# A Mamba layer and linear attention on one core: the C product taken once per four scans

## The chip, the cores and the metric

The kernel runs on one core of a Trainium2 chip. The core has a matrix engine (TensorE, PE in the profile), a vector engine (VectorE, DVE), an activation engine (ScalarE, ACT), a general engine (GpSimd, POOL) and a queue engine that here only issues DMAs (SyncE, SP). Each engine takes its instructions strictly in the order in which the program gives them, and waits for the others through semaphores. The metric is the device time of one execution in microseconds (us); the median of three runs of the kernel before is 8079.81 us.

## What is computed

`x` has 4 images of 512 channels and 4096 positions. Layer 0 normalises it, cuts the channels into 4 chunks of 128 and sends each chunk through a Mamba block, along the 4096 positions. Its core is a recurrence for each of 256 inner channels `d` and 16 states `s`:

```
dA = exp(dt_t[:, :, None] * A)
h  = dA * h + (dt_t * x_t)[:, :, None] * B_t[:, None, :]
y  = einsum('bds,bs->bd', h, C_t)
```

The y of all positions, plus a skip term, is gated, projected, normalised and projected again, and added to x. Layer 1 is a linear attention over the result (relu of q and k, k·q summed over the positions, then the output projection). Both layers are fp32.

## The kernel before

**Steps and slots.** The work is cut into 128 steps: 4 images x 8 tiles of 512 positions x 4 chunks. A step has 16 slots (`SLOTS`), numbered s = 0 to 15 here, and a slot has two scans: the recurrence over 512 positions for a block of 128 pairs of channel and state, one instruction each. Two slots make a group of four scans that shares four states; a group has one tile `h` of four rows of 512 columns, of which two buffers exist. The first slot of a group is even, the second odd. Below, "scan 4a" and "scan 4b" are the two scans of slot 4, and "P4" is slot 4's C product.

**What one slot needs.** `dA` is made by ScalarE into PSUM (`decay`, L709, three buffers, given out three scans ahead). `bx`, the input term of a slot's two scans, is made by GpSimd (`drive`, L718, three buffers, two slots ahead). VectorE runs the scans (L740). Then h must be multiplied by C. C is split by columns: for the first 384 of the 512 columns (`CUT`) TensorE spreads the C rows of the group's four states over the partitions into a PSUM tile `c_all` (`c_row`, L703, one buffer), and VectorE multiplies (`product`, L758, L763); for the last 128 columns the rows come by DMA into `c_sb`, and GpSimd multiplies all four rows of h at once (L751), after it has copied the state at the end of the scans (`st`, L750). Last, TensorE adds the product up over the states into `y` (`fold_states`, L769), eight matmuls for a group, in PSUM.

**The order.** It is written out by hand: the function `slot` (L726) gives a slot's instructions to the engines, and calls `after()` (L1114) at its end. `after()` gives out a share of all other work: the softplus of the next step at s = 3 (two table loads on ScalarE around it), the silu at s = 10 (again two), TensorE's input projections at s = 3 and 5 to 9, and pieces of the layer norms, the output projection and the attention, as many as a credit of matmul work per slot allows. The wide VectorE instructions of the layer norms (2048 columns) come at s = 3 and s = 10 (`AWAY`).

**Where the product stands.** A product takes one slot: two rows of 384 columns, 768 in all. It is given out one scan late: slot g's product follows the first scan of slot g + 1, and with it, if g is odd, the C rows of the next group and the state sums of this one. In slots 4 and 11 (`BEHIND`) the slot's own product comes as well, at its end, so these two slots have two products, the second just behind the scan that it reads, and slots 5 and 12 have none.

**PSUM and its one C tile.** Since `c_all` has one buffer, TensorE may write the next group's C rows only when VectorE has done the group's second product, and the next product needs them.

Of the kernel before, what the change touches and what calls it, by code (L numbers as in the profile page):

```python
# [11 lines left out]
ALU = mybir.AluOpType  # L12
# [12 lines left out]
def kernel(  # L25
# [24 lines left out]
    nc = tc.nc  # L50
# [7 lines left out]
    CUT = T - T // 4  # L58
# [3 lines left out]
    NJ = P // BLK  # L62
# [58 lines left out]
    def mm(out_, lhsT, rhs, abreast=1, **how):  # L121

        work["mm"] += (0.25 if rhs.dtype == BF16 else 1.0) * rhs.shape[-1] / T / abreast
        nc.tensor.matmul(out_, lhsT, rhs, **how)  # L124
# [3 lines left out]
    def diagonal(out_, w, rhs):  # L128

        for k in range(P // BLK):  # L130
            r = slice(k * BLK, (k + 1) * BLK)
            mm(out_[r, :], w[r, :], rhs[r, :], abreast=P // BLK, start=True, stop=False)
# [242 lines left out]
    def bc(v, n):  # L375
        return v.unsqueeze(1).to_broadcast([P, n, v.shape[-1]])
# [296 lines left out]
    JJ = NJ // 2  # L673
    SLOTS = NH * NQ * JJ
    AWAY = (3, 10)
    BEHIND = [s + 1 for s in AWAY]

    def place(g):

        n, r = divmod(g, SLOTS)  # L680
        e, r = divmod(r, NQ * JJ)
        return n, e, *divmod(r, JJ)

    b_all, c_all, c_sb, dAs, bxs, hs, ys = {}, {}, {}, {}, {}, {}, {}
# [8 lines left out]
    def b_row(g):  # L693
        n, e, q, _ = place(g)
        b_all[g // JJ] = wk.tile([P, T], F32, tag="b_all", name=f"b_all_{g}", bufs=3)
        for_states(b_all[g // JJ], fs[n]["b_rows"], q)

    def c_tail(g):
        n, e, q, _ = place(g)
        c_sb[g // JJ] = wk.tile([P, T - CUT], F32, tag="c_sb", name=f"c_sb_{g}", bufs=2)  # L700
        for_states(c_sb[g // JJ], fs[n]["c_rows"], q)

    def c_row(g):  # L703
        n, e, q, _ = place(g)
        got = ps_c.tile([P, CUT], F32, tag="c", name=f"c_all_{g}")
        mm(got, sel[:, q, :], fs[n]["parts"], start=True, stop=True)
        c_all[g // JJ] = got

    def decay(k):  # L709

        n, e, q, jj = place(k // 2)
        j = jj * 2 + k % 2
        dAs[k] = ps_d.tile([P, T], F32, tag="dA", name=f"dA_{k}")
        nc.scalar.activation(  # L714
            dAs[k], fs[n]["d_all", e][:, 0, j, :], AF.Exp, scale=a_t[:, e, j, q : q + 1]
        )

    def drive(g):  # L718

        n, e, q, jj = place(g)  # L720
        bxs[g] = wk.tile([P, 2, T], F32, tag="bx", name=f"bx_{g}", bufs=3)
        nc.gpsimd.tensor_tensor(  # L722
            bxs[g], fs[n]["d_all", e][:, 1, jj * 2 : jj * 2 + 2, :], bc(b_all[g // JJ], 2), ALU.mult
        )

    def slot(g, last, after):  # L726
        n, e, q, jj = place(g)
        b, t, c = steps[n]
        if g + 2 < last:
            drive(g + 2)  # L730
        if jj == 0:
            if g + 3 * JJ < last:
                b_row(g + 3 * JJ)
            hs[g // JJ] = wk.tile([P, NJ, T], F32, tag="h", name=f"h_{g}", bufs=2)
        elif g + 1 < last:
            c_tail(g + 1)
        h = hs[g // JJ]
        for i in range(2):
            j = jj * 2 + i
            nc.vector.tensor_tensor_scan(  # L740
                h[:, j, :], dAs.pop(2 * g + i), bxs[g][:, i, :],
                0.0 if t == 0 else st[:, c, e, q, j : j + 1], ALU.mult, ALU.add,
            )
            if 2 * g + i + LEAD < 2 * last:
                decay(2 * g + i + LEAD)
            if i == 0 and g and (g - 1) % SLOTS not in BEHIND:
                product(g - 1, last)
        del bxs[g]
        if jj == JJ - 1:
            nc.gpsimd.tensor_copy(st[:, c, e, q, :], h[:, :, T - 1])  # L750
            nc.gpsimd.tensor_tensor(  # L751
                h[:, :, CUT:], h[:, :, CUT:], bc(c_sb.pop(g // JJ), NJ), ALU.mult
            )
        if g % SLOTS in BEHIND:
            product(g, last)
        after()

    def product(g, last):  # L758


        _, _, _, jj = place(g)
        own = hs[g // JJ][:, jj * 2 : jj * 2 + 2, :CUT]
        nc.vector.tensor_tensor(own, own, bc(c_all[g // JJ], 2), ALU.mult)  # L763
        if jj == JJ - 1:
            if g + 1 < last:
                c_row(g + 1)
            fold_states(g)

    def fold_states(g):  # L769

        n, e, q, _ = place(g)
        if q == 0:
            ys[n, e] = ps_y.tile([P, T], F32, tag="y", name=f"y_{n}_{e}")
            diagonal(ys[n, e], dg[:, e, :], fs[n]["xz"][:, 0, e, :])
        h = hs.pop(g // JJ)
        for j in range(NJ):
            mm(
                ys[n, e][j * BLK : (j + 1) * BLK, :], fold, h[:, j, :],
                start=False, stop=(q == NQ - 1), abreast=NJ,
            )  # L780
# [232 lines left out]
    N = len(steps)  # L1013
# [86 lines left out]
    with tc.manual_schedule():  # L1100
        credit, seen, mix, held[0], held_x[0] = 0.0, work["mm"], iter(()), 0, 0
        for n, (b, t, c) in enumerate(steps):
# [10 lines left out]
            for s in range(SLOTS):  # L1113
                def after():  # L1114
# [62 lines left out]
                    seen = work["mm"]  # L1177

                slot(n * SLOTS + s, N * SLOTS, after)
            fs[n - 1].clear() if n else None  # L1180
        product(N * SLOTS - 1, N * SLOTS)
        now[0] = None
        for _, what in due:
            what()
# [60 lines left out]
```

## Time and profile before

| | value |
|---|---|
| median of 3 runs | 8079.81 us (8078.26 to 8084.43) |
| the profiled execution, its span | 8075.2 us |
| before the loop of slots, the loop, after it | 123, 7485, 468 us |
| one slot, mean (7485 / 2048) | 3.65 us |
| one scan, mean of L740 with `st` | 1271 ns |
| one C product on VectorE (L763) | 935 ns, 2048 of them |
| one `bx` on GpSimd (L722) | 2371 ns, 2048 of them |
| one C product of the tail on GpSimd (L751) | 1270 ns, 1024 of them |

The profile is of one execution. "Busy" sums the durations of an engine's instructions; neighbours on VectorE overlap by some 85 ns, so what an instruction takes of the engine's time is read as the distance from its start to the start of the next, in the timeline. A bracket in a timeline line gives the idle time before the instruction and what ended it.

### The profile page before, as it was taken

The page shows a single profiled execution, that of the slowest core. Times are in us where ns is not written, and L with a number is a line of the kernel's source. Part 1 is how long each engine was busy: PE and PEld are TensorE (multiplying, and loading weights), DVE is VectorE, ACT ScalarE, POOL GpSimd, SP SyncE. Part 2 cuts the span into 40 slices and gives each one's busy share as a digit, 9 for nine tenths or more (in the row PEclk, how much of TensorE's full clock was granted, in tenths as well). Part 3 has the DMA queues.
Part 4 walks back from the last instruction along what each step waited for, and adds up shares of the span by engine and source line. Part 5 has one row for each costly group of instructions (what it writes and reads, how often), then busy time and mean ns, then how long its engine had stood idle before and what let it go on. Part 6 is the DMA issues. An engine that isn't in the chain of part 4 may idle for free.

```text
span 8075.2 us, 92673 instructions
## 1 busy us (share of the span) xinstructions
PE 6509.7 (81%) x24880; PEld 2130.1 (26%) x24880; DVE 7049.8 (87%) x6790; ACT 5543.1 (69%) x8321; POOL 6890.9 (85%) x4597
## 2 busy tenths in 40 slices
PE   5677777667788888887788888888788888888599
PEld 1111212111223222332222222322122222322144
DVE  5999999999999989989999999998989999998600
ACT  4667777777777677777777767777776777777421
POOL 4999999999989888989998889898989999889600
PEclk7787888888899999898899999999889999999799
DMA  5666666666666666676766666677666666677402
GB/s 158 165 168 163 148 152 154 157 157 165 169 171 161 146 155 160 172 188 170 173 152 168 165 151 157 156 183 186 159 159 155 159 154 150 155 189 186 114 32 89
DMA packets 829200, 1266.00 MB, mean 157 GB/s; under 512 B 183912, under 2 KB 317560, under 8 KB 816384
## 3 DMA queue, kind: packets, MB, share of 16 engines
q1 hardware_dynamic: 804736, 1222.32, 60.3%
q0 software_dynamic: 16896, 33.56, 2.4%
q10 hardware_dynamic: 7040, 4.20, 0.2%
q8 instruction: 195, 3.19, 0.2%
q14 instruction: 333, 2.73, 0.1%
HBM read 1052.78 MB, written 206.57 MB: 156 GB/s over the span
## 4 chain that ended last, share of the span: by engine, by line
DVE 21%; PE 19%; DMA 17%; POOL 14%; issue 10%; ACT 9%; SPq 8%; POOLq 0%; DVEq 0%; ACTq 0%
DVE h L740 13%; POOL bx L722 10%; DMA d_all<-d_rows 10%; DVE h L763 6%; PE pq L124 5%; SPq L689 5%; ACT dA L714 4%; PE pc L124 3%; DMA b_all<-b_rows 3%; SPq L639 3%; PE y L124 2%; PE pr L124 2%; POOL h L751 2%; DMA c_sb<-c_rows 2%; PE pp L124 1%
## 5 line engine op out<-in xcount | busy, mean ns | idle before, releaser
L722 POOL TENSOR_TENSOR bx<-d_all,b_all 128x1024 f32<-128x1024 f32 x2048 | 4819.3, 2371 | 64.6 <-DVE h L740 48.0
L740 DVE TENSOR_TENSOR_SCAN h<-dA,st,bx 128x512 f32<-128x512 f32 x3584 | 4431.9, 1271 | 114.8 <-ACT dA L714 105.0
L714 ACT ACTIVATE dA<-d_all,a_t 128x512 f32<-128x512 f32 x4096 | 2779.7, 689 | 1761.3 <-DVE h L740 1720.6
L763 DVE TENSOR_TENSOR h<-h,c_all 128x768 f32<-128x768 f32 x2048 | 1914.8, 935 | 328.6 <-PE c_all L124 320.4
L124 PE MATMUL y<-h,fold 128*32 128x512 f32 x8192 | 1264.7, 693 | 196.6 <-POOL h L751 193.0
L751 POOL TENSOR_TENSOR h<-h,c_sb 128x512 f32<-128x512 f32 x1024 | 1300.2, 1270 | 131.9 <-DMA c_sb<-c_rows 43.3
L124 PE MATMUL pc<-xn,w_cv 128*128 128x512 f32 x2048 | 1075.2, 660 | 170.6 <-DVE xn L414 106.3
L124 PE MATMUL c_all<-parts,sel 128*128 128x384 bf16 x1024 | 368.4, 360 | 1015.4 <-DVE h L763 1014.1
L124 PE MATMUL pq<-w_qk,xa 128*128 128x512 f32 x2048 | 988.3, 615 | 1.6 <-ACT xa L367 1.6
L740 DVE TENSOR_TENSOR_SCAN h<-dA,bx 128x512 f32<-128x512 f32 x512 | 602.9, 1209 | 66.1 <-ACT dA L714 59.3
L124 PEld LDWEIGHTS pc<-xn,w_cv 128*128 128x128 f32 x2048 | 396.2, 204 | 806.4 <-issue 445.3
L124 PEld LDWEIGHTS <-sel 128*128 128x128 bf16 x1280 | 126.9, 99 | 1672.7 <-DVE h L763 1440.8
L750 POOL COPY st<-h 128x4 f32<-128x4 f32 x1024 | 209.4, 204 | 407.6 <-DVE h L740 379.4
L124 PEld LDWEIGHTS pq<-w_qk,xa 128*128 128x128 f32 x2048 | 401.6, 198 | 462.8 <-issue 443.3
L124 PE MATMUL pr<-xb,m 128*128 128x512 f32 x1024 | 494.3, 620 | 5.5 <-DMA xb<-x 4.1
L124 PE MATMUL pp<-xn,w_pr 128*128 128x512 f32 x1024 | 486.3, 601 | 3.8 <-DVE xn L414 3.8
L124 PEld LDWEIGHTS y<-h,fold 128*32 128x32 f32 x8192 | 170.1, 114 | 784.6 <-POOL h L751 323.6
L124 PE MATMUL y<-xz,dg 32*32 32x512 f32 x2048 | 338.7, 737 | 0.0
L787 POOL TENSOR_TENSOR xz<-xz 128x512 f32<-128x512 f32 x256 | 325.9, 1273 | 2.7 <-ACT xz L784 2.7
L628 POOL TENSOR_TENSOR dt<-dt,xz 128x1024 f32<-128x1024 f32 x128 | 302.4, 2362 | 23.2 <-ACT dt L620 23.1
L124 PE MATMUL pd<-xz,w_xp 128*128 128x512 f32 x512 | 305.4, 727 | 7.8 <-ACT xz L1054 7.8
L838 ACT ACTIVATE kq<-pq 128x512 f32<-128x512 f32 x256 | 150.5, 588 | 228.3 <-PE pq L124 226.9
(179 smaller groups left out, 6131.0 us busy)
## 6 DMA issues: line engine op xcount, KB each, us to landing
d_all<-d_rows SPq DMA_DIRECT2D x2048, 256.0 KB, 6.6
b_all<-b_rows SPq DMA_DIRECT2D x4096, 64.0 KB, 2.2
d_rows<-dt SPq DMA_DIRECT2D x256, 512.0 KB, 3.6
c_sb<-c_rows SPq DMA_DIRECT2D x4096, 16.0 KB, 1.9
xs<-in_x_dram SPq DMA_DIRECT2D x32, 1024.0 KB, 5.9
xn<-in_x_dram SPq DMA_DIRECT2D x32, 1024.0 KB, 5.7
xr<-in_x_dram POOLq DMA_DIRECT2D x32, 1024.0 KB, 10.7
x<-xr SPq DMA_DIRECT2D x32, 1024.0 KB, 4.2
```

What stands on the lines that cost most here:

```text
L124: nc.tensor.matmul(out_, lhsT, rhs, **how)
L628: nc.gpsimd.tensor_tensor(f["both"][:, 1], f["both"][:, 0], f["xz"][:, 0], ALU.mult)
L639: nc.sync.dma_start(d[k * BLK : (k + 1) * BLK, v], src)
L689: nc.sync.dma_start(dst[k * BLK : (k + 1) * BLK, :], rows_[q * KS + k, :].partition_broadcast(BLK))
L714: nc.scalar.activation(dAs[k], fs[n]["d_all", e][:, 0, j, :], AF.Exp, scale=a_t[:, e, j, q : q + 1])
L722: nc.gpsimd.tensor_tensor(bxs[g], fs[n]["d_all", e][:, 1, jj * 2 : jj * 2 + 2, :], bc(b_all[g // JJ], 2), ALU.mult)
L740: nc.vector.tensor_tensor_scan(h[:, j, :], dAs.pop(2 * g + i), bxs[g][:, i, :], 0.0 if t == 0 else st[:, c, e, q, j : j + 1], ALU.mult, AL ...
L750: nc.gpsimd.tensor_copy(st[:, c, e, q, :], h[:, :, T - 1])
L751: nc.gpsimd.tensor_tensor(h[:, :, CUT:], h[:, :, CUT:], bc(c_sb.pop(g // JJ), NJ), ALU.mult)
L763: nc.vector.tensor_tensor(own, own, bc(c_all[g // JJ], 2), ALU.mult)
L787: nc.gpsimd.tensor_tensor(f["xz"][:, 1, e, :], f["xz"][:, 1, e, :], f["xz"][:, 0, e, :], ALU.mult)
L838: nc.scalar.activation(qk[i], pq, AF.Relu)
```

## The change

The product is taken once for a group, over all four rows (1536 columns), at the end of the group's second slot. The C rows of the next group and the state sums stay where they were on TensorE's queue: behind the first scan of the next slot. (With the product before them in VectorE's order, they now come one scan after it; the group of slots 10 and 11, whose sums were given out at the end of slot 11, now has them in slot 12.) `BEHIND` is gone, and nothing is placed differently at s = 3 and 10. The number of scans, of `bx`, of DMAs, of matmuls and of ScalarE's instructions is the same, and the order on SP, POOL and ACT is unchanged.

```
-    BEHIND = [s + 1 for s in AWAY]
...
-            if i == 0 and g and (g - 1) % SLOTS not in BEHIND:
-                product(g - 1, last)
+            if i == 0 and jj == 0 and g:
+                fold_states(g - 1, last)
         del bxs[g]
         if jj == JJ - 1:
             nc.gpsimd.tensor_copy(st[:, c, e, q, :], h[:, :, T - 1])
             nc.gpsimd.tensor_tensor(
                 h[:, :, CUT:], h[:, :, CUT:], bc(c_sb.pop(g // JJ), NJ), ALU.mult
             )
-        if g % SLOTS in BEHIND:
-            product(g, last)
+            own = h[:, :, :CUT]
+            nc.vector.tensor_tensor(own, own, bc(c_all.pop(g // JJ), NJ), ALU.mult)
         after()
 
-    def product(g, last):
-
-
-        _, _, _, jj = place(g)
-        own = hs[g // JJ][:, jj * 2 : jj * 2 + 2, :CUT]
-        nc.vector.tensor_tensor(own, own, bc(c_all[g // JJ], 2), ALU.mult)
-        if jj == JJ - 1:
-            if g + 1 < last:
-                c_row(g + 1)
-            fold_states(g)
-
-    def fold_states(g):
+    def fold_states(g, last):
 
         n, e, q, _ = place(g)
+        if g + 1 < last:
+            c_row(g + 1)
         if q == 0:
...
-        product(N * SLOTS - 1, N * SLOTS)
+        fold_states(N * SLOTS - 1, N * SLOTS)
```

## The prediction

> **What bounds the kernel now.** I read the engines' busy shares first, then cut the span into start, loop and end, then VectorE's waits, then the timeline of one step.
>
> ```profile
> PE 6509.7 (81%) x24880; PEld 2130.1 (26%) x24880; DVE 7049.8 (87%) x6790; ACT 5543.1 (69%) x8321; POOL 6890.9 (85%) x4597
> ```
>
> ```profile
> 123.00:7608.00 7485.00, 6020.88 (x23241) 1908.48 (x23241) 6986.20 (x6625) 5406.03 (x8111) 6875.43 (x4576) 0.89 0.66 163
> ```
>
> The second line is the loop of slots: length, then busy PE, PEld, DVE, ACT, POOL. VectorE is busy for 6986 of 7485 us (93%) and GpSimd for 6875 (92%): two engines close to their limits, VectorE first. So what counts is VectorE's 500 idle microseconds, and what an instruction takes of it.
>
> ```profile
> DVE h L763 <- PE c_all L124: 320.4, 172, 6.0
> DVE h L740 <- ACT dA L714: 164.3, 104, 48.2
> DVE h L740 <- POOL bx L722: 13.4, 18, 2.2
> ```
>
> These are VectorE's longest waits inside the loop: total, times, longest. The C product's wait for `c_all` leads. By the product's place in its step, counted along VectorE's timeline of the whole loop, 222 us of waiting stand before P4, 55 before P6, 20 before P8, 17 before P14, 10 elsewhere: P4, whose C rows TensorE writes only after P3, one scan earlier. One such step (3603.37 is the end of scan 3b):
>
> ```profile
> 3601.24 0.93 DVE L763 TENSOR_TENSOR h<-h,c_all 128x768 f32<-128x768 f32 x1
> 3602.09 1.28 DVE L740 TENSOR_TENSOR_SCAN h<-dA,st,bx 128x512 f32<-128x512 f32 x1
> 3607.81 0.95 DVE L763 TENSOR_TENSOR h<-h,c_all 128x768 f32<-128x768 f32 x1 [4.45 <-PE c_all L124]
> 3608.68 3.63 DVE L740 TENSOR_TENSOR_SCAN h<-dA,st,bx 128x512 f32<-128x512 f32 x3
> ...
> 3630.00 2.27 DVE L428 TENSOR_TENSOR xn<-xn,mu_a 128x2048 f32<-128x2048 f32 x1
> 3632.18 1.28 DVE L740 TENSOR_TENSOR_SCAN h<-dA,st,bx 128x512 f32<-128x512 f32 x1
> 3633.38 0.93 DVE L763 TENSOR_TENSOR h<-h,c_all 128x768 f32<-128x768 f32 x1
> 3634.22 1.28 DVE L740 TENSOR_TENSOR_SCAN h<-dA,st,bx 128x512 f32<-128x512 f32 x1
> 3635.54 0.95 DVE L763 TENSOR_TENSOR h<-h,c_all 128x768 f32<-128x768 f32 x1
> 3636.41 3.63 DVE L740 TENSOR_TENSOR_SCAN h<-dA,st,bx 128x512 f32<-128x512 f32 x3
> 3639.95 0.93 DVE L763 TENSOR_TENSOR h<-h,c_all 128x768 f32<-128x768 f32 x1
> ```
>
> The first four lines show a product held for 4.45 us. The others give prices, start to start: a scan 1.20 (3632.18 to 3633.38; three in 3.54), a product 0.84 (3633.38 to 3634.22), and a product that reads the scan just before it starts 1.32 after that scan (3634.22 to 3635.54, P11), so 0.13 later than one with a scan between. The wide operation of 2048 columns, of the product's kind, takes 2.18.
>
> ScalarE in the same stretch:
>
> ```profile
> 3603.59 1.28 ACT L1133 ACT_TABLE_LOAD   x1
> 3604.89 1.27 ACT L620 ACTIVATE dt<-pt,dtb 128x512 f32<-128x512 f32 x2
> 3606.17 1.28 ACT L1135 ACT_TABLE_LOAD   x1
> 3607.47 1.52 ACT L367 ACTIVATE xn<-xn,off_a,gr_a 128x512 f32<-128x512 f32 x2
> 3608.90 1.28 ACT L714 ACTIVATE dA<-d_all,a_t 128x512 f32<-128x512 f32 x2
> ```
>
> It gives no `dA` from before the table load until 3609.57. That is the next limit where P4's wait goes.
>
> **What the Trainium skill says.** "Perfetto Trace Analysis", section "Optimizing Scalar/DVE Operations": each VectorE operation on PSUM has about 125 ns of overhead, and larger operations help a saturated engine. Here the trace has less: from 768 and 2048 columns, (2.18 - 0.84) / 1280 = 1.047 ns a column, and 0.84 - 768 x 1.047 = 0.04 us is fixed. "VectorE: DVE Perf Modes", section "The DRAIN you can't avoid": a read of what the instruction before wrote needs a semaphore or an instruction between; it holds that the semaphore costs nothing extra. The trace differs: 0.13 us, and the measurement decides. "GPSIMD Engine Reference", section "Key points": GpSimd contends with VectorE instructions that have two SBUF inputs; the product has one, its other input is PSUM, so I leave `bx` at 2371 ns.
>
> **The change part by part.**
>
> *One product in place of two.* 1536 columns take 0.04 + 1536 x 1.047 = 1.65 against 2 x 0.845 = 1.69: 0.045 less, x1024 groups = -46 us. With the skill's 125 ns it would be -128.
>
> *The product right behind its scan.* Each of 1024 now waits for the last scan to be written: 0.13 x 1024 = +133 us. P4 and P11 paid it before: 256 x 0.13 = 33. So +100. Together VectorE's own work grows by 100 - 46 = +54; with 0.14 for the wait and scans 0.02 dearer behind a scan than ahead of a product, as medians over the loop have it, by up to +80. I take +65, and +60 of it on the path, since part lies in VectorE's idle time behind the silu of slot 10. Bounds: -30 (the skill's overhead) and +80.
>
> *The wait for the C rows.* TensorE gets the next C rows and the sums at the same place of its queue, but the product that they wait for now stands before scan a of that slot. The rows have four scans until the next product reads them, 4.8 us, where P4 gave them one, 1.2. In the step shown they were ready at 3607.8, and the new product, four scans behind one that ends at 3605.1, would not ask before 3609.9. All 324 us go, but for a few.
>
> *What is late next.* In the step shown: scan 3b ends at 3603.37, the product of four rows at 3605.1, scans 4a, 4b, 5a at 3608.7; scan 5b needs the `dA` that ends at 3609.57. It starts there instead of at 3608.68 + 2 x 1.19 = 3611.06: of 4.45 us, 1.5 stay. Over the 128 steps I compared P4's wait with how long scan 5b's `dA` had been ready before it started (same timeline, ends on ACT, starts on DVE), taking the smaller: 174 of 222 us are not stopped by `dA`. Carrying this on scan by scan to 10b with the later `dA` and with `bx`, and adding the waits at P6 and P8: 150 to 155 us reach slot 10. The waits elsewhere leave 28. So about 180 of 324 pass.
>
> ScalarE's reach is otherwise unchanged. Between scan b of a slot and the fourth scan after it, where `dA` given out behind that slot's `after()` is needed, VectorE has three scans and two products' worth of columns before and after the change, whichever slot it is: 5.4 us. The lead of three buffers covers what it covered, the silu of slot 10 included.
>
> *TensorE.* `c_row` no longer waits for a scan and a product after the group (2.05 us behind its last scan), but for the big product (1.78); the sums need GpSimd's tail too, 0.2 + 0.08 + 1.27 behind the scan. So PE's 1014 us of waiting for L763 shrinks by 0.3 us a group. It is not the bound on the whole, but is busy for 20.4 of 23.6 us in slots 4 to 9 of that step:
>
> ```profile
> 3603.40:3627.00 23.60, 20.44 (x76) 6.95 (x77) 16.52 (x16) 17.46 (x27) 17.87 (x13) 1.00 0.79 224
> ```
>
> I count nothing for its being earlier, 0 to -40. A wide operation at s = 3 comes behind the big product, up to 0.9 later, and PE's `pc` waits for it in some 60 steps (106 us now): 0 to +30, in slack that the later C rows give. I take 0.
>
> *GpSimd.* Its order and its DMAs stay. Its floor in the loop is 6875 plus 0.13 of dependent gap in each of 1024 pairs `st`, L751, about 7000; the loop would have to lose 480 us to meet it. Queues: no DMA is added or moved, on SP or POOL.
>
> Sum: +60 - 180 = -120 on 8075.2, a span of 7955. The runs lie 4.6 above the span: 7960 us.
>
> **The rivals.** *All of the wait pays* (C rows never late, and ScalarE, fed earlier by TensorE, not in the way): 324 - 60 = 264 off, 7816. For it: the `dA` that stops scan 5b is itself late at times because ScalarE waited for TensorE, as for `pr` at 3602.89 in this step. Against: the table loads, 2.6 us in each softplus, do not move.
>
> *Nothing stays* (the +60 eats what passes): 60 to 80 us pass; 8080, within 0.2% (16 us, what a measurement can tell).
>
> *Slower: TensorE's backlog comes back elsewhere.* In slots 4 to 9 PE, at 87% and more, sets the pace, and the C wait was only where it showed. VectorE then runs ahead by a slot, the relu and residual copies on ScalarE wait for PE in front of the `dA`, and scans wait for `dA`. The 324 return as waits on L714, and the longer chain on VectorE stays: +60, 8140. It decides once less than 60 / 324, a fifth, passes. For it: in the loop ACT already waits some 250 us for PE (`y` 80, `pp` 46, `pq` 33, `pr` 30, sums of the norms 62). Against: those waits are 3.6 us at the longest, and at most scans `dA` has been ready for 2 us.
>
> *The change does not do what it says*: the built order has 1024 products of 4 x 384 columns directly behind scan b, each with a wait on VectorE and one on PE; excluded.
>
> **How the numbers follow.** Forecast 0.54, own range 7900 to 8040 (150 to 220 pass by a cost of 45 to 80, and PE's 40); all pays 0.14; nothing stays 0.08; slower 0.24. Faster by over 0.2%: 0.54 + 0.14 = 0.68; same 0.08; slower 0.24. The range holds the forecast and no change, most of the full gain, and reaches into the slower case until about 0.2 is left out: 7850 to 8110.
>
> **What would show it.** L763: 1024 times, about 1740 ns (935 + 768 x 1.047), starting 1.32 behind its scan's start; its wait for `c_all` under 40 us; L740's wait for `dA` up from 164 to some 300. It would be wrong if L740's wait for `dA` or `bx` took over 400 us, or a wait of L740 for `y` (1.6 us now) became large, for then h's buffers, and PE, set the pace.

## The result: 0.6% faster, less than half of what was forecast

The changed kernel takes 8030.8 us (median of 4 runs, 8026.5 to 8040.0), the kernel before 8079.0 in the same comparison: a ratio of 0.9942, 95% interval 0.9927 to 0.9956. That is 48 us less, where 120 were forecast, and the time lies inside the range. The profiled execution has a span of 8024.7 us, 50.5 below that of before. All of it is in the loop of slots, which now lasts 7434 us (before 7485); what stands ahead of it and behind it is unchanged.

The windows of the loop after, columns as in the line of before (length, busy PE, PEld, DVE, ACT, POOL, TensorE's clock, DMA):

```profile
123.00:7557.00 7434.00, 6015.21 (x23241) 1910.74 (x23240) 6985.98 (x5601) 5409.39 (x8112) 6871.33 (x4576) 0.89 0.66 164
```

VectorE has 1024 instructions fewer, and is busy for as long as before (6986 us both times). The 51 us come out of its idle time. Of its waits in the loop after, those on the recurrence and its product (total, times, longest):

```profile
DVE h L739 <- ACT dA L713: 264.1, 175, 46.7
DVE h L754 <- PE c_all L124: 88.9, 76, 3.0
DVE h L739 <- POOL bx L721: 4.3, 6, 1.7
```

The wait for the C rows fell by 231 us (320 to 89), the scans' wait for `dA` rose by 100 (164 to 264): 54 of them at slot 5, 21 at slot 7, 13 at slot 12, counted along VectorE's timeline. A third change is in no list of waits between engines; it shows in the groups (busy, mean ns, idle before, what ended it):

```profile
L754 DVE TENSOR_TENSOR h<-h,c_all 128x1536 f32<-128x1536 f32 x1024 | 1796.9, 1755 | 189.8 <-PE c_all L124 88.9 <-DVE h L739 2.3 <-PE y L124 0.5
```

The product stands idle for 189.8 us, of which the C rows explain 88.9. The other 101 are nearly all pieces of 0.1 us, before 941 of the 1024 products; before the change this rest was 8 us (328.6 less 320.4). The timeline of VectorE after shows them:

```profile
3585.26 4.80 DVE L739 TENSOR_TENSOR_SCAN h<-dA,st,bx 128x512 f32<-128x512 f32 x4
3590.17 1.75 DVE L754 TENSOR_TENSOR h<-h,c_all 128x1536 f32<-128x1536 f32 x1
3591.84 3.63 DVE L739 TENSOR_TENSOR_SCAN h<-dA,st,bx 128x512 f32<-128x512 f32 x3
3600.49 1.28 DVE L739 TENSOR_TENSOR_SCAN h<-dA,st,bx 128x512 f32<-128x512 f32 x1 [5.02 <-ACT dA L713]
```

Four scans end at 3585.26 + 4.80 = 3590.06, and the product starts at 3590.17, 0.11 later. An instruction that doesn't need the one just ahead of it, and is not kept waiting, starts some 0.085 before that one has ended, as the scan at 3591.84 does (the product ends at 3591.92). So the product loses both: the 0.11 and the overlap.

The last line shows where a C wait went. It is the same step as in the prediction: P4 waited for 4.45 us before, and now scan 5b waits for 5.02. ScalarE in that stretch:

```profile
3593.78 0.69 ACT L975 ACTIVATE res<-pr,ob 128x512 f32<-128x512 f32 x1 [2.98 <-PE pr L124]
3594.48 1.28 ACT L1123 ACT_TABLE_LOAD   x1
3595.78 1.27 ACT L620 ACTIVATE dt<-pt,dtb 128x512 f32<-128x512 f32 x2
3597.06 1.28 ACT L1125 ACT_TABLE_LOAD   x1
3598.36 1.52 ACT L367 ACTIVATE xn<-xn,off_a,gr_a 128x512 f32<-128x512 f32 x2
3599.78 1.28 ACT L713 ACTIVATE dA<-d_all,a_t 128x512 f32<-128x512 f32 x2
```

It waits 2.98 us for TensorE, does the softplus between two table loads, and gives the `dA` for 5b at 3600.45. From the end of scan 3b (3590.06) to 5b it is 10.4 us here and was 10.3 before (3599.53 to 3609.87): in this step nothing was won.

TensorE in that stretch, after the change, and then its C rows before the change:

```profile
3594.52 1.98 PE L124 MATMUL pc<-xn,w_cv 128*128 128x512 f32 x4 [0.78 <-ACT res L975]
3596.52 1.98 PE L124 MATMUL pr<-xb,m 128*128 128x512 f32 x4
3598.34 0.33 PE L124 MATMUL c_all<-parts,sel 128*128 128x384 bf16 x1
```

```profile
3607.45 0.33 PE L124 MATMUL c_all<-parts,sel 128*128 128x384 bf16 x1
```

The product ends at 3591.92, but the C rows start only at 3598.34. On TensorE's queue they stand behind a piece of the input projection (`pc`), which waits for ScalarE's `res`, and behind `pr`. They start 3.87 us after `res` has ended. Before the change P3 ended at 3602.17, `res` at 3603.58, and the rows started at 3607.45, again 3.87 us after `res`. In this step it was TensorE's own queue that held the rows, with the change and without it, and not the product. It is no exception. In the kernel before, the rows for slots 4 and 5 start within 0.4 us of P3's end in 19 of the 128 steps, after the change within 0.4 us of the product's end in 14.

### The profile page after: what moved, and what is told of

Its sections match the earlier page's. It is cut to its first block, busy times and chain, and to the rows that moved or that the text cites. A ratio compares the mean times of both kernels' runs of the same rounds, so it can differ in the third digit from the quotient of the medians.

```text
span 8024.7 us, 91633 instructions
## 1 busy us (share of the span) xinstructions
PE 6503.6 (81%) x24880; PEld 2132.3 (27%) x24880; DVE 7050.9 (88%) x5766; ACT 5545.6 (69%) x8321; POOL 6886.8 (86%) x4597
## 4 chain that ended last, share of the span: by engine, by line
PE 29%; DVE 27%; ACT 22%; issue 8%; DMA 6%; POOL 3%; SPq 2%; DVEq 0%; POOLq 0%; ACTq 0%
DVE h L739 24%; ACT dA L713 9%; PE pc L124 8%; PE pq L124 5%; PE y L124 4%; DMA d_all<-d_rows 3%; PE po L124 3%; PE pp L124 3%; PE pr L124 3%; ACT xz L1044 2%; POOL bx L721 2%; SPq L688 2%; ACT L1145 1%; ACT L1044 1%; ACT L1123 1%
## 5 line engine op out<-in xcount | busy, mean ns | idle before, releaser
L721 POOL TENSOR_TENSOR bx<-d_all,b_all 128x1024 f32<-128x1024 f32 x2048 | 4827.4, 2367 | 283.6 <-DVE h L739 268.0
L739 DVE TENSOR_TENSOR_SCAN h<-dA,st,bx 128x512 f32<-128x512 f32 x3584 | 4330.9, 1265 | 207.7 <-ACT dA L713 196.3
L754 DVE TENSOR_TENSOR h<-h,c_all 128x1536 f32<-128x1536 f32 x1024 | 1796.9, 1755 | 189.8 <-PE c_all L124 88.9
L124 PE MATMUL pc<-xn,w_cv 128*128 128x512 f32 x2048 | 1107.0, 677 | 255.8 <-ACT dt L620 156.8
L124 PE MATMUL pq<-w_qk,xa 128*128 128x512 f32 x2048 | 968.8, 606 | 2.2 <-ACT xa L367 2.2
L124 PE MATMUL pz<-xn,w_z 128*128 128x512 f32 x512 | 273.9, 627 | 8.8 <-DVE kq L835 3.3
```

Of the source, the lines that this page charges most:

```text
L721: nc.gpsimd.tensor_tensor(bxs[g], fs[n]["d_all", e][:, 1, jj * 2 : jj * 2 + 2, :], bc(b_all[g // JJ], 2), ALU.mult)
L739: nc.vector.tensor_tensor_scan(h[:, j, :], dAs.pop(2 * g + i), bxs[g][:, i, :], 0.0 if t == 0 else st[:, c, e, q, j : j + 1], ALU.mult, AL ...
L754: nc.vector.tensor_tensor(own, own, bc(c_all.pop(g // JJ), NJ), ALU.mult)
```

## The experiments

Times are medians of 4 runs or more, ratios are against the kernel before in the same comparison.

**One scan later: the product not behind its own scan.** The instruction stays; only its place moves behind the first scan of the next slot.

```
             if i == 0 and jj == 0 and g:
+                product(g - 1)
                 fold_states(g - 1, last)
...
-            own = h[:, :, :CUT]
-            nc.vector.tensor_tensor(own, own, bc(c_all.pop(g // JJ), NJ), ALU.mult)
...
+    def product(g):
+        own = hs[g // JJ][:, :, :CUT]
+        nc.vector.tensor_tensor(own, own, bc(c_all.pop(g // JJ), NJ), ALU.mult)
...
+        product(N * SLOTS - 1)
         fold_states(N * SLOTS - 1, N * SLOTS)
```

> The product over 1536 columns stays one instruction per group, but is given out behind the first scan of the next slot, with the C rows and the state sums behind it. Theory A (the gain fell short because each product waits for the scan just before it: 1.36 us from that scan's start to the product's in the profile of after, against 1.175 with no wait, 0.19 x 1024 = 194 us of VectorE): product starts 1.18 behind the scan ahead of it, its idle time under 40 us, time 7850 to 7930. Theory B (ScalarE's dA sets the pace, and what VectorE gains it loses again in waits of L739 for dA): time 8000 to 8035, with the wait for dA up from 264 us to over 400.

7950.6 us, ratio 0.9838 (0.9823 to 0.9852): 80 us better than the change, and better than both kernels. Groups, loop and timeline of VectorE (the loop's columns as before):

```profile
L758 DVE TENSOR_TENSOR h<-h,c_all 128x1536 f32<-128x1536 f32 x1024 | 1767.8, 1726 | 0.1
```

```profile
123.00:7475.00 7352.00, 5955.48 (x23212) 1892.74 (x23240) 6910.08 (x5601) 5369.04 (x8111) 6862.65 (x4577) 0.90 0.67 166
```

```profile
3577.83 4.80 DVE L739 TENSOR_TENSOR_SCAN h<-dA,st,bx 128x512 f32<-128x512 f32 x4
3582.55 1.73 DVE L758 TENSOR_TENSOR h<-h,c_all 128x1536 f32<-128x1536 f32 x1
3584.19 2.45 DVE L739 TENSOR_TENSOR_SCAN h<-dA,st,bx 128x512 f32<-128x512 f32 x2
```

The idle time of the product is 0.1 us in all; it starts at 3582.55, before the scan ahead has ended (3582.63), and takes 1.64 of the engine's time to the next start (1.67 after the change). Busy VectorE time in the loop falls from 6986 to 6910. So the place behind its own scan cost 101 + 76 = 177 us of VectorE: the cost of the place is shown. Not all of it is time, for other waits took some of it; those in the loop are now

```profile
DVE h L739 <- ACT dA L713: 224.8, 179, 46.7
DVE h L739 <- PE y L124: 81.1, 81, 3.4
DVE h L739 <- POOL bx L721: 74.4, 70, 4.2
```

The C wait is gone from the product, since the first scan, which waits until TensorE has summed up (`y`) and so freed h's buffer, waits for a matmul behind those C rows. That wait, 81 us, and GpSimd's `bx`, 74, take their share, while the wait for `dA` falls from 264 to 225. The time falls between the two expectations.

**No slot with two products, products of 768 columns.** The kernel before, `BEHIND` removed and nothing else.

```
-            if i == 0 and g and (g - 1) % SLOTS not in BEHIND:
+            if i == 0 and g:
                 product(g - 1, last)
...
-        if g % SLOTS in BEHIND:
-            product(g, last)
```

> The kernel before, with P3, P4, P10 and P11 each one scan late like all others (no slot with two products). Theory A (the wait of before was made by the two products of slot 4, with one scan between P3 and P4 for the C rows): the wait for c_all falls from 320 us to 100 to 160, and the 256 products behind their own scan are gone (33 to 45 us); time 7980 to 8030, as good as the change itself. Theory B (the wait goes only because the rows have four scans in place of two or one): wait still over 250 us, time 8050 to 8080.

8035.6 us, ratio 0.9942 (0.9927 to 0.9956): the very ratio of the change. Neither theory is right in full: the time is near A's, but the C wait is still 259 us, as in B.

```profile
DVE h L760 <- PE c_all L124: 259.0, 174, 5.4
```

Along the timeline 111 us of it stand before P4, which now comes in slot 5, and 107 before P6 in slot 7; they were 222 and 55. Against the kernel before there are 61 us less of C wait, 8 less of busy VectorE and 6 less of short gaps before products, but 20 more of waiting for `dA` and 10 for `bx`. So in this kernel the longer instruction, placed at the end of its slots, earned nothing over short ones that all come one scan late. Where both come one scan late, the long one is 85 us faster (7950.6): there its rows have four scans, here two. How much of the 85 comes from that, and how much from the joining, was not separated.

**Two products, the second at its own slot's end.**

```
+            if i == 0 and jj == 1:
+                product(g - 1)
             if i == 0 and jj == 0 and g:
                 fold_states(g - 1, last)
...
-            own = h[:, :, :CUT]
-            nc.vector.tensor_tensor(own, own, bc(c_all.pop(g // JJ), NJ), ALU.mult)
+            product(g)
...
+    def product(g):
+        jj = place(g)[3]
+        own = hs[g // JJ][:, jj * 2 : jj * 2 + 2, :CUT]
+        nc.vector.tensor_tensor(own, own, bc(c_all[g // JJ], 2), ALU.mult)
```

> Two products of 768 columns per group: the first behind the first scan of the odd slot, the second at the odd slot's end, behind its own scan; rows and sums as in after. If the dependent product costs more where it has to wait for PE as well (two semaphores), the second product here, whose rows the first one waited for, starts 1.31 behind its scan and not 1.36; then against after: -0.05 x 1024 for the wait, +0.02 x 1024 for the second instruction, and the rows have three scans in place of four: 8000 to 8030. If the extra belongs to the length of the product, it starts 1.36 behind its scan here too: 8030 to 8060.

8181.6 us, ratio 1.0122 (1.0106 to 1.0137), slower than the kernels above and outside both expectations. VectorE's timeline has a product of each kind:

```profile
3630.69 0.93 DVE L761 TENSOR_TENSOR h<-h,c_all 128x768 f32<-128x768 f32 x1
3631.67 1.28 DVE L739 TENSOR_TENSOR_SCAN h<-dA,st,bx 128x512 f32<-128x512 f32 x1
3632.99 0.95 DVE L761 TENSOR_TENSOR h<-h,c_all 128x768 f32<-128x768 f32 x1
```

The second product starts 1.32 behind its scan; the long one of the changed kernel 1.36 (median of 1024; the median here is 1.31). What differs is that the long one has two semaphores to wait for, its scan's and the C rows'; here the first product has waited for the rows. Counted from the end of the scan, this is 0.035 here and 0.105 there. Other products of the record leave only the pair of waits as the cause. In the kernel before, P4 has both waits and is a short product: where its rows were early (35 of 128 times), it starts 0.105 after its scan. In the next run below, 43 of the 1024 long products have no wait for TensorE: they start 0.035 after their scan, the other 981 mostly 0.105. The trace also shows where the time goes: with two waits, the one for the scan stands in a wait instruction of its own (EVENT_SEMAPHORE) ahead of the product. It starts 0.039 after the scan's end, and the product 0.066 later (medians).

The time is another matter. The C wait is 314 us over the whole loop, against 89 after the change, and that is what my expectation had wrong: with the product of the even slot behind scan a of the odd one, the rows again have to be there two scans after they are given out. The granted clock of TensorE is a little lower here (0.883, after the change 0.894); what that adds was not separated.

**C rows and sums at the end of the slot.** They are given out right behind the product, ahead of `after()`.

```
             nc.vector.tensor_tensor(own, own, bc(c_all.pop(g // JJ), NJ), ALU.mult)
+            fold_states(g, last)
...
-            if i == 0 and jj == 0 and g:
-                fold_states(g - 1, last)
...
-        fold_states(N * SLOTS - 1, N * SLOTS)
```

> As after, but the C rows and the state sums are given to TensorE right behind the product, ahead of the slot's other work, and so wait at the head of TensorE's queue for product and GpSimd's tail. If giving them one scan later is worth something by itself, this is slower than after: TensorE stands about 1.7 us at each odd slot's end, up to 0.5 us of it on the path: 8100 to 8300. If TensorE's place for them doesn't matter: 8020 to 8045.

8207.8 us, ratio 1.0157 (1.0140 to 1.0174), as the first expectation had it. VectorE no longer waits for C rows, but over the whole loop it waits 466 us for `dA` (264 after the change), and ScalarE waits longer for TensorE: 315 us for `pc` against 56, 125 for `pq` against 75. TensorE in turn waits 1254 us for the product, against 874. So it is worth 177 us to give out the rows and sums one scan behind the product, as the change leaves them; given out at once, they hold at the head of TensorE's queue what ScalarE needs next.

**More softplus: is ScalarE's block on the path?** One of the two softplus instructions of slot 3 is done twice, in the kernel before, the changed one and the one-scan-later one.

```
+        nc.scalar.activation(
+            f["both"][:, 0, 1, :], f["pt"][1], AF.Softplus, bias=dtb[:, 1:2]
+        )
```

> The kernel before with one softplus of slot 3 done twice (0.67 us more on ScalarE in each of 128 steps, 86 us in all). Theory A of the prediction (in the kernel before the C rows hold P4, ScalarE's dA comes next only when that wait is gone): mostly hidden, 8080 to 8105. Rival B (the softplus already holds the C rows, because TensorE's input projection stands ahead of them and waits for the PSUM bank that the softplus reads): the wait for c_all rises by 30 to 70 us, time 8120 to 8165.

> The changed kernel with the same softplus done twice, 86 us more on ScalarE. Theory A (scan 5b waits for the dA behind the softplus, 75 us at slot 5 now): the wait for dA rises by 30 to 70 us, time 8065 to 8100, against hardly anything before. If ScalarE's block does not matter: 8025 to 8045.

> The product one scan later (7951 us) with one softplus of slot 3 done twice, 86 us more on ScalarE. If ScalarE's block before scan 5b limits there as it does in the changed kernel, where the same cost 39 to 47 us of 86: 7985 to 8010, with the waits for dA up by 40 to 60. If GpSimd or TensorE has taken its place (waits for bx and y are up by some 150 us there): 7950 to 7975.

Before: 8089.7 us, ratio 1.0010 (1.0003 to 1.0017), 6 us more than the 8083.4 beside it; the C wait rises from 320 to 336 (in an execution of 8099 us), less than rival B had it. Changed kernel: 8077.8, ratio 0.9990 (0.9981 to 0.9999), 39 (by the ratios) to 47 us (by the medians) more than without. One scan later: 7966.4, ratio 0.9855 (0.9840 to 0.9870), 16 more, inside the second expectation, though its wait for `dA` rises from 225 to 263. VectorE's waits for `dA` in the first two (the same view):

```profile
DVE h L743 <- ACT dA L717: 182.0, 114, 46.3
```

```profile
DVE h L742 <- ACT dA L716: 309.3, 179, 46.7
```

Before the change the 86 us of added ScalarE work are mostly hidden; after it about half of them are time. The wait for `dA` at slot 5 rises from 21 to 41 in the first and from 75 to 121 in the second. So the next limit that the prediction named at scan 5b is there, and became one by the change.

**The first projection piece one slot later on TensorE.**

```
-                    if s in (3, 5, 6, 7, 8, 9):
+                    if s in (4, 5, 6, 7, 8, 9):
                         next(front, None)
```

> The changed kernel with the first piece of the input projection given to TensorE at slot 4 in place of slot 3, so that nothing that waits for the softplus's PSUM bank stands ahead of the C rows for slots 4 and 5. If that bank is what keeps the C rows late (76 waits, 89 us, 22 at slot 5 and 54 at slot 7) and holds PE (157 us of pc waiting for the softplus): waits for c_all under 40 us, time 7980 to 8015. If the C rows are late because PE simply has too much work in slots 4 to 9: 8025 to 8050.

> The product one scan later (7951 us) with the first piece of the input projection at slot 4. If PE's bank wait is also behind the 81 us that scans wait for y there: 7905 to 7935; if not: 7945 to 7970.

On the changed kernel 8042.6 us, ratio 0.9949 (0.9935 to 0.9964): not faster. On the one-scan-later kernel 8110.7, ratio 1.0035 (1.0022 to 1.0048), 160 worse than without, against both expectations. In the first the C wait is halved and `dA` takes it over:

```profile
DVE h L739 <- ACT dA L713: 318.8, 187, 46.7
DVE h L754 <- PE c_all L124: 43.3, 45, 4.0
```

The rows do come earlier at slot 5: those for slots 4 and 5 are written 1.8 us after the product ahead of them (median), against 4.8 after the change, and the wait there is 0.2 us for 22. So the piece ahead of them on TensorE's queue was what kept these rows late. It brought no time: 46 us less of the one wait are 55 more of the other. Since the same move puts more work on TensorE from slot 4 on, this run doesn't say what the PSUM bank costs by itself.

In the second the wait of scans for `y` is 197 us for 81, 141 of them at slot 8, and the wait for `dA` 326 for 225. It fits that the work moved into TensorE's full slots made its sums, and with them the buffers of h, late. The granted clock is lower too (0.878 for 0.898), and what that adds was not separated.

**Less work for TensorE at slot 4.** The Mamba block's skip term is left out; the credit still counts it.

```
         po = f["po"] = work_bank(f"po_{nm}", 0)
-        diagonal(po, skd, xn[:, c, NTAP - 1 : NTAP - 1 + T])
+        work["mm"] += 1.0
         for e in range(NH):
-            mm(po, w_op[:, e, :], f["xz"][:, 1, e, :], start=False, stop=(e == NH - 1))
+            mm(po, w_op[:, e, :], f["xz"][:, 1, e, :], start=(e == 0), stop=(e == NH - 1))
```

> The changed kernel without the eight small matmuls of the Mamba block's skip term at slot 4 (the skip_scale term is left out; the credit counts them still, so that all other work stays in its slot). They take TensorE about 1.06 us a step, 136 us in all, ahead of the C rows of slots 6 and 7. If the C rows are late because TensorE has too much work from slot 4 on: the wait for c_all falls from 89 to 30 to 60 us and the time by 15 to 50, to 7980 to 8015. If TensorE's load there is no limit: 8020 to 8040.

8005.9 us, ratio 0.9906 (0.9889 to 0.9922), 25 less than the changed kernel, as expected of a load that limits. The C wait falls less than expected, from 89 to 69. At slot 7 it falls from 54 to 28, and the rows for slots 6 and 7 are written 3.0 us after the product (median) in place of 4.0; at slot 5, ahead of the work left out, it stays at 22. So about half of the C wait at slot 7 is TensorE's load in slot 4. The rest of it stays open.

## Why the forecast gain was too high, step by step

*What bounds the kernel*: right as to the place. The C wait of P4 was the largest idle time of VectorE in the loop, and went. The reason given for it, that P3 stands only one scan ahead, fits few steps: in 109 of 128 the rows started over 0.4 us after P3's end, held by other work on TensorE's queue where the result's lines show it.

*One product in place of two, -46 us*: the size came out only where the product is not held. One scan later it takes 1.646 (1.65 worked out, median); held behind its scan 1.672, so the change saved 20.

*The product right behind its scan, +100*: mis-sized, the first of two terms. The price of 0.13 was read from P11, which waits for its scan alone; the new product waits for its scan and for the C rows, and starts 1.364 behind its scan, not 1.31, 0.19 over the 1.175 of a product that is not held. I had taken both changes on VectorE as +65, +60 of it on the path. Measured as VectorE's own time, busy the same and the product's idle rest 8 to 101, it is +93. My upper bound was 80. The +80 counted on dearer scans, but they became cheaper: a scan behind a scan takes 1.175 from start to start, before the change 1.194 (medians), some 35 us in all. Without that the cost would have been higher still. Why they did is open.

*The wait for the C rows, "All 324 us go, but for a few"*: the second mis-sized term, and here the step itself failed. 89 us stayed, 22 of them at slot 5 and 54 at slot 7, where before P6 had waited 55. I had counted scans between the giving out of the rows and the product, four of 4.8 us. But being given out is not being written: TensorE writes the rows for slots 4 and 5 about 4.8 us after the product (median) and those for slots 6 and 7 about 4.0 us after it, since other work stands ahead of them on its queue. The run with the projection piece moved shows it for slot 5, the run without the skip term for about half of slot 7. I had looked at TensorE's load there, 20.4 of 23.6 us, and used it only for the slower rival.

*What is late next*: right in kind and near in size. `dA` rose to 264 us ("some 300"), at slot 5 from 21 to 75, where the prediction's comparison over all steps (222 less 174) left 48 to come back. But its example was misread by one slot. The lines just ahead of those shown there:

```profile
3598.25 1.28 DVE L740 TENSOR_TENSOR_SCAN h<-dA,st,bx 128x512 f32<-128x512 f32 x1
3600.04 1.28 DVE L740 TENSOR_TENSOR_SCAN h<-dA,st,bx 128x512 f32<-128x512 f32 x1 [0.51 <-PE y L124]
```

These are scans 3b and 4a. The scan at 3602.09 is 4b, with P3 ahead of it and P4 behind, and not 3b; 3b ended at 3599.53, and 5b started at 3609.87, 0.3 after its `dA`. In that step nothing could pass, and nothing did. The C rows were misread with it. Counted from 3599.53, and with the prediction's own prices (1.73 and 4.8), the product of four rows ends at about 3601.3 and the next one, were no `dA` late, asks at about 3606.1, which is 1.7 before the rows of 3607.8: rightly read, the example spoke against "all 324 us go". The sums over 128 steps counted slots from the start of the loop and are not touched by this. With a place read wrongly, an example proves the opposite of what it shows.

*The sum.* Waits that went: 231 - 100 + 9 (`bx`) = 140, where 180 were forecast to pass. Costs: 93 for 60. 140 - 93 = 47, and the loop became 51 shorter. The other 4 are in smaller waits. With either of the two terms right, this sum would have come to 80 to 87.

*GpSimd*: as said; it is busy for 6871 us (6875), its `bx` 2367 ns (2371). That it would only bind after 480 us was too far: in the one-scan-later kernel, with the loop 133 us shorter, `bx` already holds VectorE for 74 us.

*The rivals.* "Slower" named the right mechanism, TensorE's backlog coming back as waits on `dA`; in the changed kernel 89 us of C wait stayed and the wait for `dA` rose by 100, in the kernel with rows at the slot's end all came back and more. How much of the 100 is TensorE's backlog and how much ScalarE's table loads is not shown. It stopped short of deciding, since 140 of 324 passed, more than a fifth.

## What to carry to other kernels

Joining two instructions saves one start, here 0.045 us; putting the joined one straight behind the instruction whose result it reads cost up to 0.19 each time, four times as much, and one independent instruction between them is enough to have both. A price for a wait must be read from an instruction that waits for the same number of things: here a second one cost 0.07. And what is given out early is not yet done early: look at what stands on the queue of the engine that is waited for, not only at the distance between the two instructions.

## What was not expected of the hardware

- A VectorE instruction that waits for the one just ahead of it starts 0.035 us after that one's end when this is its only semaphore (two-product run, P11 before, 43 long products of the run with rows at the slot's end), and 0.105 after it when it waits for TensorE's semaphore too, though that one had been given (changed kernel, P4 before). Both numbers stand for short and for long products, so it is the second wait and not the length. The extra 0.07 is a wait instruction of its own, which comes between the two. Where the scan waited for is not the one just ahead, two waits cost nothing: so for the first products of the two-product run, which start 0.08 before the end of the scan ahead of them.
- A held instruction also takes longer to the next start: 0.872 for 0.846 at 768 columns, 1.672 for 1.646 at 1536. The Trainium skill ("VectorE: DVE Perf Modes", section "The DRAIN you can't avoid") has a semaphore after each of eight copies cost nothing extra; here starting late and taking longer were together 0.16 to 0.22 a time.
